# Rotated FFN: the residual added by an accumulating transfer from DRAM instead of by POOL

## The chip, the core and the metric

The kernel runs on one core of a Trainium2 chip. The metric is the device time of one execution in microseconds (us); the time of a kernel is the median of its runs. The engines are named as in the profile: PE (matmul), PEld (its weight loads), DVE (VectorE), ACT (ScalarE), POOL (GpSimd) and SP (SyncE, which only issues transfers here).

## The reference, cut to what matters

The program is one block of a network on `x` of 128 batches of 32 rows of 512 numbers, that is 4096 rows: cross-attention with a residual, then a delta-rule attention block with its own MLP and a residual, and at the end the stage that the change is in, a feed-forward network (FFN) with quantised and Hadamard-rotated activations:

```python
def h_bitlinear(x, w):
    xq = act_quant(fwht(x))      # Hadamard rotation, then 8-bit rounding by the row's maximum
    wq = weight_quant(w)         # weights rounded to -1, 0, 1 times one scale
    return jnp.einsum('bsh,oh->bso', xq, wq)
...
gate = h_bitlinear(hidden_states, w_gate)       # 512 -> 2048
up = h_bitlinear(hidden_states, w_up)           # 512 -> 2048
return h_bitlinear(jax.nn.silu(gate) * up, w_down)   # 2048 -> 512
...
x = x + _L0_ffn_ref(_layernorm(x, axis=-1), L0_ffn_w_gate, L0_ffn_w_up, L0_ffn_w_down)
```

The last line is the one concerned: the `x` ahead of the plus sign is the residual.

## The kernel before, in words

`perceiver_block` runs the stages one after the other: `cross_attention`, `delta_products`, `delta_out_mlp`, `hadamard_ffn`. The MLP stage writes two arrays of 4096 x 512 to DRAM: `x2`, the residual stream, and `z2`, the same rows with their mean taken off and the first part of the Hadamard rotation done. `hadamard_ffn` reads both and writes `out`.

`hadamard_ffn` works on 32 tiles of 128 rows, in a software pipeline of three tiles. In turn `i` of its loop (line 1055) it does, in the order of the program:

- it loads `z` of tile `i+3` (`zt`, four buffers) and turns `z` of tile `i+1` on PE (`turned`, L97, copied by ACT at L970);
- it loads `x2` of tile `i` (`xt`, four buffers) by `load` (L932), through SP's queue;
- it starts the gate and up products of tile `i` (`middle`: PE L996 and L999, ACT's SiLU at L1001, DVE's product at L1002), and between them rounds tile `i+1` (`integers`: DVE's maximum at L976, the scale `qs` by L948 to L951, ACT's rounding `t` at L956, DVE at L960);
- it turns the middle result of tile `i-1` (`middle_turned`), rotates it on PE (`rotated`, L939), finds its maximum (DVE L1016, L1020) and rounds it (`last_integers`, ACT L956 and L958, DVE L960, and the factor `fd` at L1026);
- it turns the integers of tile `i-2` and multiplies them with the last weights (`finish`: 16 matmuls at L1039). ACT scales the product into `xo` (L1041, three buffers), POOL adds `xt` to it (L1042), and a DMA on POOL's queue stores `xo` to `out` (L1043);
- at the end DVE does the rest of the rotation of tile `i`, eight adds and subtractions on 128 x 1024 numbers, ping-pong between the tiles `m` and `mb` (`butterflies`, L126 and L127).

The order in which each engine executes its instructions isn't this order: a scheduler of the language arranges them by priority and by its own estimate of when operands are ready, so that butterflies lie between the short steps of the rounding. Waits between engines, buffers and transfers are made by the language. PSUM has eight buffers in this stage, shared by all products (`ps`). The buffers of a stage are laid on the memory that earlier stages let go, and wait for it tile by tile.

Of the kernel before, what the change touches and what calls it, by code (L numbers as in the profile page):

```python
# [13 lines left out]
ALU = mybir.AluOpType  # L14
# [4 lines left out]
P = 128  # L19
# [99 lines left out]
def butterflies(nc, a, b):  # L119

    n = a.shape[1] // P
    step = 1
    while step < n:
        i = a.rearrange("p (a c d) -> p a c d", c=2, d=step * P)
        o = b.rearrange("p (a c d) -> p a c d", c=2, d=step * P)
        nc.vector.tensor_add(o[:, :, 0, :], i[:, :, 0, :], i[:, :, 1, :])  # L126
        nc.vector.tensor_sub(o[:, :, 1, :], i[:, :, 0, :], i[:, :, 1, :])  # L127
        a, b, step = b, a, 2 * step
    return a
# [769 lines left out]
def hadamard_ffn(g: Ctx, x2, z2, mv2, had, ffn, out):  # L899


    tc, nc = g.tc, g.nc
# [7 lines left out]
    with tc.tile_pool(name="d_w", **right) as wp, tc.tile_pool(name="d_w2", **right) as wp2, stack:  # L910
# [19 lines left out]
        def load(i, src, name):  # L930
            t = xp.tile([P, D], FP, name=name)
            nc.sync.dma_start(t, src[i * P : (i + 1) * P, :])  # L932
            return t

        def rotated(xT, c0):

            pr = ps.tile([P, D], FP, name="ps")
            for c in range(DC):
                nc.tensor.matmul(  # L939
                    pr[:, c * P : (c + 1) * P], xT[:, c0 + c, :], hd, start=True, stop=True  # L940
                )
            return pr
# [19 lines left out]
        def statistics(ns):  # L962

            nc.scalar.activation(rstd[:, ns], mv2[:, ns, 1], AF.Sqrt, bias=g.ln_eps)
            nc.vector.reciprocal(rstd[:, ns], rstd[:, ns])
            nc.vector.tensor_scalar_mul(rstd[:, ns], rstd[:, ns], c1)

        def turned(i):
            zT = wk1.tile([P, DC, P], FP, name="zT")
            nc.scalar.copy(zT, g.transposed(ps, z.pop(i), g.ident))  # L970
            return zT

        def integers(i, pr):

            mx = st.tile([P, 1], FP, name="mx")
            nc.vector.tensor_reduce(mx, pr, AX.X, ALU.max, apply_absolute_value=True)  # L976
            m, qs = scales(mx, rstd[:, i : i + 1])
            q = wk1.tile([P, D], BF, name="q")
            rounded(q, pr, qs)
            f = st.tile([P, 2], FP, name="f")  # L980
            nc.vector.tensor_scalar_mul(f, both, m)
            return q, f

        def integers_turned(q, f):
            qT = wk1.tile([P, DC, P], BF, name="qT")
            nc.scalar.copy(qT, g.transposed(ps, q, g.identb, BF))
            return qT, f

        def middle(qT, f):

            m = mp.tile([P, IF], FP, name="m")
            for k in range(NG):
                ks = slice(k * D, (k + 1) * D)
                pg = ps.tile([P, D], FP, name="ps")
                for dc in range(DC):
                    nc.tensor.matmul(pg, qT[:, dc, :], wg[:, dc, ks], start=dc == 0, stop=dc == DC - 1)  # L996
                pu = ps.tile([P, D], FP, name="ps")
                for dc in range(DC):
                    nc.tensor.matmul(pu, qT[:, dc, :], wu[:, dc, ks], start=dc == 0, stop=dc == DC - 1)  # L999
                s = wk.tile([P, D], FP, name="s")  # L1000
                nc.scalar.activation(s, pg, AF.Silu, scale=f[:, 0:1])  # L1001
                nc.vector.scalar_tensor_tensor(m[:, ks], pu, f[:, 1:2], s, ALU.mult, ALU.mult)  # L1002
                yield m

        def middle_turned(m):
            mT = mp.tile([P, IC, P], FP, name="mT")
            for k in range(NG):
                pt = g.transposed(ps, m[:, k * D : (k + 1) * D], g.ident)
                nc.scalar.copy(mT[:, k * DC : (k + 1) * DC, :], pt)
            return mT  # L1010

        def last_integers(pr):

            mx = st.tile([P, NG], FP, name="mx4")
            for k in range(NG):
                nc.vector.tensor_reduce(  # L1016
                    mx[:, k : k + 1], pr[k], AX.X, ALU.max, apply_absolute_value=True
                )
            mx1 = st.tile([P, 1], FP, name="mx")
            nc.vector.tensor_reduce(mx1, mx, AX.X, ALU.max)  # L1020
            mm, qs = scales(mx1, c2)
            q = mp1.tile([P, IF], BF, name="q2")
            for k in range(NG):
                rounded(q[:, k * D : (k + 1) * D], pr[k], qs, k % 2 == 0)
            f = st.tile([P, 1], FP, name="fd")
            nc.vector.tensor_mul(f, mm, sd)  # L1026
            return q, f

        def last_turned(q):
            qT = mp1.tile([P, IC, P], BF, name="q2T")  # L1030
            for k in range(2):
                pt = g.transposed(ps, q[:, k * IF // 2 : (k + 1) * IF // 2], g.identb, BF)
                nc.scalar.copy(qT[:, k * IC // 2 : (k + 1) * IC // 2, :], pt)  # L1033
            return qT

        def finish(i, x, qT, f):
            pd = ps.tile([P, D], FP, name="ps")
            for c in range(IC):
                nc.tensor.matmul(pd, qT[:, c, :], wd[:, c, :], start=c == 0, stop=c == IC - 1)  # L1039
            xo = wk.tile([P, D], FP, name="xo")  # L1040
            nc.scalar.activation(xo, pd, AF.Copy, scale=f)  # L1041
            nc.gpsimd.tensor_add(xo, xo, x)  # L1042
            nc.gpsimd.dma_start(out[i * P : (i + 1) * P, :], xo)  # L1043

# [2 lines left out]
        rstd = wp.tile([P, n], FP, name="rstd")  # L1049
        z = {i: load(i, z2, "zt") for i in range(3)}  # L1050
        nc.sync.dma_start(wd.rearrange("p c n -> p (c n)"), ffn[2][0])
        x = {}
        statistics(slice(0, late))
        f, m, q = integers_turned(*integers(0, rotated(turned(0), 0))), {}, {}
        for i in range(n + 2):
            if i + 3 < n:
                z[i + 3] = load(i + 3, z2, "zt")
            if i + 1 < n:
                zT = turned(i + 1)
            if i < n:  # L1060
                x[i] = load(i, x2, "xt")
                steps = middle(*f)
                m[i] = next(steps)
            if i == n // 2:
                statistics(slice(late, n))
            if i + 1 < n:
                f = integers(i + 1, rotated(zT, 0))
            if i < n:
                for _ in steps:
                    pass  # L1070
            if 0 <= i - 1 < n:
                mT = middle_turned(m.pop(i - 1))
            if 0 <= i - 2:
                q2, fd = q.pop(i - 2)
                q2T = last_turned(q2)
            if 0 <= i - 1 < n:
                q[i - 1] = last_integers([rotated(mT, k * DC) for k in range(NG)])
            if i + 1 < n:
                f = integers_turned(*f)
            if 0 <= i - 2:  # L1080
                finish(i - 2, x.pop(i - 2), q2T, fd)
            if i < n:
                m[i] = butterflies(nc, m[i], mp.tile([P, IF], FP, name="mb"))

# [2 lines left out]
def perceiver_block(  # L1087
# [26 lines left out]
    with tc.tile_pool(name="s_l", bufs=1, side="right", reuse_waits="tile") as sp:  # L1114
# [9 lines left out]
        def beside_mlp(b):  # L1124
# [9 lines left out]
            x2, z2, mv2, beside_mlp,  # L1134
        )
    hadamard_ffn(g, x2, z2, mv2, had, list(zip(fq, scales)), out)


# [57 lines left out]
```

## Time and profile before

| what | us |
|---|---|
| median of 3 runs | 3079.94 |
| lowest and highest run | 3078.09, 3083.41 |
| the profiled execution | 3080.81 |
| its span | 3079.0 |
| first turn of the FFN on PE | 2414.96 |
| first and last POOL add | 2470.26, 3069.38 |
| PE busy over the whole span | 2934.2 |
| DVE busy over the whole span | 2059.5 |
| ACT busy over the whole span | 1090.1 |
| POOL busy over the whole span | 706.0 |

The span is the profiled execution from its first to its last instruction; the time around it, 1.8 us, is start and end. An engine's busy time is the time in which it executes instructions, without those that issue transfers. In the prediction, a line of a group gives line of code, engine, operation, output and input, count, then busy time and mean time of one, then the idle time of the engine just before these instructions and what ended it. The granted TensorE clock in this execution was 0.984 of full speed over the span.

### The profile page before, as it was taken

Reading aid. Unit: us, or ns where it says so; the run is one execution under the profiler, and the core shown is the slowest. Engines: PE = TensorE matmul, PEld = TensorE weight load, DVE = VectorE, ACT = ScalarE, POOL = GpSimd, SP = SyncE. Lnnn points to the kernel's source line nnn. Section 1 sums busy time; section 2 is a strip of 40 time slices with the busy share of each in tenths; the row PEclk is TensorE's granted clock in tenths of the full one; section 3 lists DMA queues with packets and bytes.
Section 4 is the critical chain, followed back from the end, with each engine's and each line's share of the span. In section 5 each row is a group of like instructions: output and inputs, shape, how many; then the busy total and the mean of one; then the engine's idle time right before and its main releaser. Section 6 shows DMA issues by size and latency. Waiting matters only on the chain.

```text
span 3079.0 us, 42048 instructions
## 1 busy us (share of the span) xinstructions
PE 2934.2 (95%) x15558; PEld 1683.7 (55%) x15558; DVE 2059.5 (67%) x3432; ACT 1090.1 (35%) x1812; POOL 706.0 (23%) x995
## 2 busy tenths in 40 slices
PE   8999999999999999599999999999999899999997
PEld 3444344443333333367676666667777566666664
DVE  2353434326699797378778787878422599999996
ACT  1111111215656666312221112111111366666665
POOL 1121212112686675321212111011000010000001
PEclk9999999999999999799999999999999999999998
DMA  9797989863554544641423323131411111111110
GB/s 332 265 311 269 307 306 310 274 213 98 166 148 131 173 129 132 198 126 59 128 74 106 97 66 112 48 101 50 139 42 42 55 42 42 42 42 35 39 31 21
DMA packets 258236, 408.09 MB, mean 133 GB/s; under 512 B 68336, under 2 KB 170864, under 8 KB 254576
## 3 DMA queue, kind: packets, MB, share of 16 engines
q1 hardware_dynamic: 223856, 305.21, 31.7%
q0 software_dynamic: 34176, 100.19, 9.5%
q8 instruction: 124, 2.03, 0.3%
q14 instruction: 80, 0.66, 0.1%
HBM read 288.36 MB, written 93.85 MB: 124 GB/s over the span
## 4 chain that ended last, share of the span: by engine, by line
PE 41%; DVE 17%; ACT 5%; issue 3%; DMA 2%; SPq 0%; POOL 0%; DVEq 0%; POOLq 0%; ACTq 0%
PE pm L834 9%; PE pm L823 9%; PE pm L826 9%; PE pp L520 5%; PE ps L797 3%; DVE mb L127 3%; ACT t L956 3%; DVE mb L126 2%; DVE mx L1016 2%; DVE m L126 2%; PE pg L455 2%; PE ps L764 2%; DVE m L1002 1%; DVE m L127 1%; DVE W L442 1%
## 5 line engine op out<-in xcount | busy, mean ns | idle before, releaser
L823 PE MATMUL pm<-hT,wg 128*128 128x256 f32 x1408 | 342.1, 386 | 0.7 <-ACT hT L812 0.7
L826 PE MATMUL pm<-hT,wu 128*128 128x256 f32 x1408 | 333.3, 379 | 0.0
L436 DVE TENSOR_TENSOR pr<-L,W 128x1984 f32<-128x1984 f32 (+30 forms) x248 | 312.1, 1258 | 24.6 <-DMA L<-ld 20.6
L442 DVE TENSOR_TENSOR W<-W,pr 128x1984 f32<-128x1984 f32 (+30 forms) x248 | 309.0, 1246 | 3.2
L834 PE MATMUL pm<-wd,mT 128*128 128x512 f32 x704 | 307.2, 592 | 0.0
L823 PEld LDWEIGHTS pm<-hT,wg 128*128 128x128 f32 x1408 | 262.2, 191 | 57.5 <-issue 16.2
L826 PEld LDWEIGHTS pm<-hT,wu 128*128 128x128 f32 x1408 | 267.2, 190 | 36.2
L834 PEld LDWEIGHTS pm<-wd,mT 128*128 128x128 f32 x704 | 132.6, 190 | 160.8 <-issue 160.7
L828 ACT ACTIVATE sg<-pm 128x256 f32<-128x256 f32 x176 | 67.4, 383 | 350.1 <-PE pm L823 340.1
L829 DVE TENSOR_TENSOR mT<-pm,sg 128x256 f32<-128x256 f32 x176 | 73.8, 419 | 164.1 <-PE pm L826 150.0
L1042 POOL TENSOR_TENSOR xo<-xo,xt 128x512 f32<-128x512 f32 x32 | 42.7, 1336 | 581.6 <-ACT xo L1041 581.6
L996 PE MATMUL ps<-wq,qT 128*128 128x512 bf16 x512 | 133.1, 383 | 28.9 <-DVE m L1002 17.3
L956 ACT ACTIVATE t<-ps,magic,qs 128x512 f32<-128x512 f32 x160 | 117.6, 777 | 96.5 <-DVE qs L951 96.4
L461 POOL TENSOR_TENSOR kk<-kk,cm 128x256 f32<-128x256 f32 x128 | 135.5, 1058 | 2.1
L999 PE MATMUL ps<-wq,qT 128*128 128x512 bf16 x512 | 132.4, 381 | 2.2 <-DVE m L1002 2.2
L458 POOL DMA_DIRECT2D ld<-kk x128 | 92.2, 720 | 147.4 <-ACT kk L457 140.4
L346 PE MATMUL ps<-hT,wq 128*128 128x512 f32 x256 | 118.6, 623 | 7.2 <-ACT hT L339 7.2
L939 PE MATMUL ps<-hd,mT 128*128 128x128 f32 x1024 | 121.5, 277 | 0.0
L455 PE MATMUL pg<-kqm,kq 128*32 128x512 f32 x896 | 118.8, 601 | 2.1 <-DMA kqm<-kq 1.5
L302 PE MATMUL ps<-wo,aoT 128*128 128x512 f32 x256 | 118.8, 608 | 1.5 <-ACT aoT L295 1.5
L520 PE MATMUL pp<-hT,wk 128*128 128x512 f32 x256 | 118.6, 604 | 0.3 <-DVE acc L527 0.3
L1039 PE MATMUL ps<-wq,q2T 128*128 128x512 bf16 x512 | 117.2, 383 | 0.9 <-ACT q2T L1033 0.9
(217 smaller groups left out, 5220.6 us busy)
## 6 DMA issues: line engine op xcount, KB each, us to landing
kall<-in_ctxT_dram SPq DMA_DIRECT2D x32, 2056.0 KB
cx<-in_ctx_dram SPq DMA_DIRECT2D x32, 2048.0 KB
x<-xo POOLq DMA_DIRECT2D x64, 256.0 KB, 3.4
xt<-x SPq DMA_DIRECT2D x64, 256.0 KB
ld<-kk POOLq DMA_DIRECT2D x128, 128.0 KB, 2.5
pd<-kk POOLq DMA_DIRECT2D x128, 128.0 KB, 2.3
L<-ld SPq DMA_DIRECT2D x8, 2048.0 KB
pe<-pd SPq DMA_DIRECT2D x256, 64.0 KB
```

The costliest lines, as they stand in the source:

```text
L126: nc.vector.tensor_add(o[:, :, 0, :], i[:, :, 0, :], i[:, :, 1, :])
L436: nc.vector.tensor_mul(pr[:, 0:n], bc(L[:, s, :, s + 1 : T].rearrange("p h t -> p t h"), HD), w[:, s].unsqueeze(1).to_broadcast([P, n, H4, ...
L442: nc.vector.tensor_sub(w[:, s + 1 :], w[:, s + 1 :], pr[:, 0:n])
L455: nc.tensor.matmul(pg[js], k[:, js], m[:, :, :, js], start=True, stop=True)
L461: nc.gpsimd.tensor_mul(kk[:, 1], kk[:, 1], cm.unsqueeze(1).to_broadcast([P, HH, T]))
L520: nc.tensor.matmul(pp.rearrange("p b t -> p (b t)"), w[n][:, dc, ec * P : (ec + 1) * P], hT[:, dc, :], start=dc == 0, stop=dc == DC - 1,)
L823: nc.tensor.matmul(pg, wg[:, dc, fs], hT[:, dc, :], start=dc == 0, stop=dc == DC - 1)
L826: nc.tensor.matmul(pu, wu[:, dc, fs], hT[:, dc, :], start=dc == 0, stop=dc == DC - 1)
L834: nc.tensor.matmul(pd, mT[:, fc, i * P : (i + 1) * P], wd[:, fc, :], start=fc == 0, stop=fc == FC - 1,)
L956: nc.scalar.activation(t, pr, AF.Identity, bias=magic, scale=qs)
L996: nc.tensor.matmul(pg, qT[:, dc, :], wg[:, dc, ks], start=dc == 0, stop=dc == DC - 1)
L999: nc.tensor.matmul(pu, qT[:, dc, :], wu[:, dc, ks], start=dc == 0, stop=dc == DC - 1)
```

## The change

`finish` no longer takes the tile `x`. After ACT has put the scaled product into `xo`, POOL's queue issues a DMA whose source is the tile's rows of `x2` in DRAM and whose destination is `xo` in SBUF, with the operation add: the DMA reads the destination and adds to it. The store of `xo` to `out` is issued by SP's queue instead of POOL's, after that transfer has landed. The add on POOL and the loads of `xt` are gone, and with them the four buffers of `xt`.

```diff
-        def finish(i, x, qT, f):
+        def finish(i, qT, f):
             pd = ps.tile([P, D], FP, name="ps")
             for c in range(IC):
                 nc.tensor.matmul(pd, qT[:, c, :], wd[:, c, :], start=c == 0, stop=c == IC - 1)
             xo = wk.tile([P, D], FP, name="xo")
             nc.scalar.activation(xo, pd, AF.Copy, scale=f)
-            nc.gpsimd.tensor_add(xo, xo, x)
-            nc.gpsimd.dma_start(out[i * P : (i + 1) * P, :], xo)
+            nc.gpsimd.dma_start(xo, x2[i * P : (i + 1) * P, :], accum_op=ALU.add)
+            nc.sync.dma_start(out[i * P : (i + 1) * P, :], xo)
...
-        x = {}
...
-                x[i] = load(i, x2, "xt")
...
-                finish(i - 2, x.pop(i - 2), q2T, fd)
+                finish(i - 2, q2T, fd)
```

## The prediction

> **What bounds the kernel now.** I began with the page's first parts. The span is 3079.0 us; POOL is busy for 23% of it, so its own work cannot be the limit. The line to be changed stands among the costly groups:
>
> ```profile
> L1042 POOL TENSOR_TENSOR xo<-xo,xt 128x512 f32<-128x512 f32 x32 | 42.7, 1336 | 581.6 <-ACT xo L1041 581.6
> ```
>
> It shows 32 adds, one for each tile of 128 rows, 42.7 us in all on an engine that waits 581.6 us for ACT in between. Taken by themselves they are worth nothing. So I asked for the engines' busy time in the steady part of this stage (columns: stretch, its length, then busy us and count of PE, PEld, DVE, ACT, POOL, then the granted clock, DMA share, GB/s):
>
> ```profile
> 2512.00:3032.00 520.00, 490.26 (x3329) 327.38 (x3328) 475.76 (x758) 331.26 (x526) 47.55 (x52) 1.00 0.12 38
> ```
>
> PE and DVE are both above 91% here, the clock is full and the DMA engines are nearly idle. Which of the two leads is told by the chain of waits in order of time, over one tile (start, us, what):
>
> ```profile
> 2567.48 2.21 DVE mb L127
> 2569.69 0.06 DVE m L948
> 2569.76 1.20 DVE m L126
> 2570.95 0.07 DVE qs L950
> 2571.03 0.06 DVE fd L1026
> 2571.09 1.04 issue
> 2572.13 0.16 DVE qs L951
> 2572.29 0.02 issue
> 2572.32 1.45 ACT t L956 x2
> ```
>
> The chain runs through DVE without a break up to the scale `qs`, from there through ACT's rounding `t`, then the SiLU `s`, and back to DVE at L1002. PE is not on it. The "1.04 issue" is no gap: in the timeline DVE runs another butterfly (L127) there. The first line is the odd one: that butterfly took 2.21 us. The groups by shape, from 2500 to 3000 us, show the same instruction against its siblings (busy, mean ns):
>
> ```profile
> L127 DVE TENSOR_TENSOR mb<-m 128x1024 f32<-128x1024 f32 x51 | 88.6, 1738 | 0.0
> L126 DVE TENSOR_TENSOR mb<-m 128x1024 f32<-128x1024 f32 x51 | 62.4, 1223 | 0.9
> L127 DVE TENSOR_TENSOR m<-mb 128x1024 f32<-128x1024 f32 x50 | 60.6, 1213 | 0.0
> ```
>
> A mean of 1738 over 51 is a mixture of 1.22 and 2.29. The timeline says which are long:
>
> ```profile
> 2587.92 1.26 POOL L1042 TENSOR_TENSOR xo<-xo,xt 128x512 f32<-128x512 f32 x1 [18.45 <-ACT xo L1041]
> 2587.97 2.29 DVE L127 TENSOR_TENSOR mb<-m 128x1024 f32<-128x1024 f32 x1
> ...
> 2589.47 0.56 POOL L1043 DMA_DIRECT2D out_dram<-xo  x1 [0.30 <-POOL xo L1042]
> ```
>
> POOL's add ends at 2589.18, and the butterfly ends 1.08 us later, which is its usual time less the overlap of pipelined instructions: it stood still while POOL read SBUF. The POOL adds start at 2488.45, 2508.06, 2527.47, 2548.04 and so on to 3043.78: 28 periods in 555.33 us, a mean of 19.83, made of 11 long ones (20.57) and 17 short ones (19.3 to 19.6). Whether PE has room is in the waits from 2500 to 3000 us (total, times, longest):
>
> ```profile
> PE ps L996 <- DVE m L1002: 17.3, 10, 1.7
> PE ps L996 <- ACT t L956: 9.6, 15, 0.7
> ```
>
> In 25 tiles PE stalls 26.9 us, 1.73 in a long period, about 0.64 in a short one, each time for a PSUM buffer that DVE or ACT releases late. So DVE bounds this stage, through ACT, and PE follows close behind.
>
> **What the Trainium skill says.** "SBUF — State Buffer", section "Who interferes with whom": a DVE instruction with two SBUF inputs and a GpSimd instruction that reads SBUF contend, and the second to issue is blocked fully until the first is done. The trace agrees: 2.29 against 1.22 us, and the order of issue is as stated (POOL 0.05 us ahead). The same section separates DMA from engine ports: DMA traffic contends with no engine, while writing the descriptors of a GpSimd DMA does need SBUF. The trace shows plain issues at L1043 (0.56 us each) beside butterflies that kept their 1.22 us. "DMA: Bandwidth & Descriptors", section "SWDGE vs HWDGE vs iDMA", says that only GpSimd issues an accumulating DMA; no such transfer is in this trace. Its section "Rules for kernel authors" says that an accumulate reads its destination and writes later, so others must wait for its semaphore: the store of `xo` therefore waits for it to land.
>
> **The change part by part.**
>
> *Removed: 32 POOL adds.* On POOL: 42.7 us, off the chain, worth 0. On DVE: the butterflies held, those of the adds from 2488.45 to 3023.11, are 28, at 2.29 - 1.22 = 1.07 us; 28 x 1.07 = 30.0. At 3043.78 the add holds L1026 instead, which takes 1.14 in place of 0.14: 1.0. The first add (2470.26) was itself the one that waited, and at the last two (3062.53, 3069.38) DVE is not in a butterfly. Sum 31.0 us, each on the chain. How much comes through? In a long period PE's stall falls from 1.73 to 0.7, so all 1.07 comes through. In a short one PE can move up only 0.64 at L996; but then its turns of `m` (L97) wait three times more for ACT, 0.23, 0.16 and 0.16 us in the timeline, 0.55 in all, which ACT's earlier `t` and `s` take away too. 0.64 + 0.55 = 1.19 is just over 1.07. I take 95%: -29.5, bounds -22 (first rival) to -31.
>
> *Removed: 32 loads of `xt` on SP*, 0.32 us of queue each, waiting for the add: worth 0, nothing waited for SP.
>
> *Added: 32 accumulating DMAs on POOL in the place of 32 plain stores.* Each waits for ACT's `xo`, as the add did; behind it on POOL is only the next tile's. `x2` was last stored at 2416.14, landing 5.2 later, before the first use at 2470. Steady cost 0 if the issue is like L1043. Unknown from both sides: from 0, if it holds nothing, to a hold of its whole length on DVE, which is the slower rival. The issue moves 1.5 us earlier, beside the same butterfly as the add; I take 0, since plain issues held none.
>
> *Moved: 32 stores from POOL to SP*, 0.32 us of queue each. SP now waits for the accumulate to land, and the next load of `zt` stands behind that wait. A `zt` buffer is one of four and is filled some three periods (59 us) before use; 8 us late costs 0. Who else waits: ACT's `xo` has three buffers; a buffer lives 0.7 + 1.7 + 3.2 = 5.6 us now, and with a landing of 4 about 0.7 + 4.3 + 3.5 = 8.5 us, of 59. That cover would be gone only at a landing above some 50 us.
>
> *The end.* Now: ACT ends `xo` at 3069.29, POOL adds, issues at 3070.93, and lands 3.2 later at 3074.1; the close-down takes the rest to 3079.0. After: issue at 3069.5; landing unknown, from 2.3 (the page's row for `z` stores) to 10.4 (its 1088 KB row); a 256 KB store to `x2` has 3.4, and I choose 4.0, since this transfer also reads what it adds to. 3073.5, SP 0.3, landing 3.2: 3077.0. That is +2.9; bounds +0.2 to +9.5.
>
> *The start.* Four `xt` buffers leave the pool, so tiles behind it lie 8 KB lower and may fall on other tiles of the MLP stage. The last of those is let go by the store at 2419.20, landing 4.1 later, 2423.3, and the first product here is at 2415: between -1 and +8; I take 0, since the first turns need only `zt`, allocated ahead of `xt`.
>
> *The order of instructions* is a scheduler's; the long and short periods differ by one butterfly ahead of L951. All short: 11 x 1.25 = -14. All long: 17 x 1.25 = +21. I take 0, because DVE's work and its data don't change.
>
> Sum: -29.5 + 2.9 = -26.6. The profiled execution took 3080.81 (span 3079.0 and 1.8 around it), so it would become 3054.2; the median shown, 3079.94, lies 0.9 lower: **3053.5 us**.
>
> **The rivals.** *PE takes over.* Only the visible stalls can go: 11 x 1.07 + 17 x 0.64 = 22.7, less 2.9: -19.8, 3060. For it: PE is busy 94%. Against it: the hidden waits at L97. *The order turns out differently*: 3040 with all periods short, 3053.5 + 21 = 3074.5 with all long. For it: small changes of timing in a scheduler move such choices. Against it: POOL and SP gate no DVE instruction. *Slower: the accumulating issue holds DVE.* Place: POOL's issue right behind `xo`, beside L127. If writing its descriptors shuts DVE out for its whole length, the cost is 31 x that length; it eats the gain of 26.6 at 0.9 us and makes the kernel measurably slower (+6.2) from about 1.1 us. At 2 us: 62 - 26.6 = +35, 3115. For it: the accumulating form is in no row and may need more descriptors. Against it: 32 plain issues held nothing.
>
> **How the numbers follow.** Forecast 0.57, PE takes over 0.19, shorter order 0.08, longer order 0.07, issue holds DVE 0.09. About 0.2%, 6.2 us, is what a measurement can tell from no change. Faster: 0.57 + 0.19 + 0.08 = 0.84; same: 0.07; slower: 0.09. The range runs from 3043, most of the way to the shorter order, to 3075, the longer order with the bounds of start and end in the forecast; the slower rival stays out.
>
> **What would show it.** Right: L127 `mb` at a mean near 1220 ns, periods near 18.3 and 19.5, PE stalls at L996 down to about 0.7 and 0, no `xt`, a tail that ends some 8 us after the last `xo`. PE takes over: DVE waits for `ps` at L1016 or L1002, PE without stalls, periods of 18.7. Wrong: L127 still long beside POOL's DMA issue; or periods unchanged with L127 short, which would say that something else than DVE set them.

## The result and the profile after

The changed kernel takes 3048.1 us (median of 4 runs, 3047.4 to 3048.8) against 3081.7 for the kernel before in the same series (3078.1 to 3083.6). The ratio is 0.9892, with a 95% interval from 0.9876 to 0.9907: 33.6 us faster by the medians. The profiled execution took 3048.66, its span is 3046.9.

The page has the line of the change first (columns as before). POOL has no add left; what L1042 now counts is the issue of a transfer:

```profile
L1042 POOL DMA_DIRECT2D xo<-x x32 | 27.1, 848 | 591.1 <-ACT xo L1041 591.1
```

An issue of the accumulating form takes 0.85 us, where the plain store at L1043 took 0.56 before. The groups by shape, from 2500 to 3000 us, are those that told of the stall before:

```profile
L126 DVE TENSOR_TENSOR mb<-m 128x1024 f32<-128x1024 f32 x54 | 66.1, 1224 | 0.9
L127 DVE TENSOR_TENSOR mb<-m 128x1024 f32<-128x1024 f32 x54 | 65.8, 1218 | 0.0
L127 DVE TENSOR_TENSOR m<-mb 128x1024 f32<-128x1024 f32 x54 | 65.7, 1217 | 0.0
```

The mixed mean of 1738 ns is gone: L127 into `mb` is as fast as its siblings. The count says the rest: 54 in 500 us in the place of 51. In the timeline the same butterfly stands beside POOL's issue and keeps its 1.21 us, in either order:

```profile
2584.80 1.21 DVE L127 TENSOR_TENSOR mb<-m 128x1024 f32<-128x1024 f32 x1
...
2584.90 0.83 POOL L1042 DMA_DIRECT2D xo<-x  x1 [18.65 <-ACT xo L1041]
...
2603.14 0.85 POOL L1042 DMA_DIRECT2D xo<-x  x1 [17.40 <-ACT xo L1041]
2603.15 1.21 DVE L127 TENSOR_TENSOR mb<-m 128x1024 f32<-128x1024 f32 x1
```

In the first pair the butterfly starts ahead of the issue, in the second behind it; neither is held.

The waits of the same stretch (total, times, longest) show what became of PE's stalls:

```profile
PE ps L996 <- DVE m L1002: 5.9, 9, 0.7
```

Before, PE stood 26.9 us there in 25 tiles. Now the short periods have no stall and the long ones 0.65 us. In the steady stretch (stretch, length, then PE, PEld, DVE, ACT, POOL, clock, DMA, GB/s) PE is busy for 98%:

```profile
2512.00:2992.00 480.00, 471.30 (x3241) 323.82 (x3290) 438.25 (x742) 325.42 (x516) 21.16 (x25) 1.00 0.18 41
```

From the fifth period on, a period (from one start of ACT's `xo` to the next) is shorter by the hold and by no more: the short and the long ones take 18.23 and 19.49 us where they took 19.31 and 20.57. PE, DVE and ACT execute the same instructions in the same order in both kernels (some 60 of PE's 4096 matmuls are missing from the later trace), so nothing of this comes from a new order. The chain of waits, useful before, is not so here: at the end it follows POOL's issues, and most of their idle time is put down to "issue".

Where the 33.1 us between the two spans' FFN stages (664.1 and 630.9, from PE's first turn of `zt` to the end of the span) lie, by the starts of `xo` (the 0.69 us of the last `xo` itself are left out):

| part | before | after | difference |
|---|---|---|---|
| PE's first turn to the first `xo` | 54.54 | 56.71 | +2.2 |
| first to thirtieth `xo`, 29 periods | 573.51 | 541.67 | -31.8 |
| thirtieth to last `xo` | 25.60 | 22.85 | -2.8 |
| end of the last `xo` to the end of the span | 9.76 | 9.01 | -0.7 |

The stage is the better measure for small differences: in the profiles of all kernels here it begins anywhere from 2405 to 2421 us, though no instruction ahead of it was changed (one kernel writes the residual stream to another place).

### The profile page after: what moved, and what is told of

Same layout as the page of the kernel before. It is cut to its first block, busy times and chain, and to the rows that moved or that the text cites. A ratio compares the mean times of both kernels' runs of the same rounds, so it can differ in the third digit from the quotient of the medians.

```text
span 3046.9 us, 41948 instructions
## 1 busy us (share of the span) xinstructions
PE 2924.9 (96%) x15496; PEld 1685.1 (55%) x15558; DVE 2030.7 (67%) x3432; ACT 1090.5 (36%) x1812; POOL 660.0 (22%) x963
## 4 chain that ended last, share of the span: by engine, by line
PE 39%; issue 23%; DVE 3%; DMA 1%; POOL 1%; ACT 0%; SPq 0%; POOLq 0%; DVEq 0%; ACTq 0%
PE pm L823 8%; PE pm L834 8%; PE pm L826 8%; PE pp L520 5%; PE ps L797 4%; PE pg L455 2%; PE ps L764 2%; DVE W L442 1%; DVE pr L436 1%; POOL xo L1042 1%; DMA wd<-in_WdownT_dram 1%; PE ps L97 1%; PE pm L455 0%; PE pn L579 0%; DMA xs<-x 0%
## 5 line engine op out<-in xcount | busy, mean ns | idle before, releaser
L1042 POOL DMA_DIRECT2D xo<-x x32 | 27.1, 848 | 591.1 <-ACT xo L1041 591.1
L996 PE MATMUL ps<-wq,qT 128*128 128x512 bf16 x509 | 131.7, 380 | 8.3 <-DVE m L1002 5.9
L999 PE MATMUL ps<-wq,qT 128*128 128x512 bf16 x484 | 126.2, 381 | 1.1 <-DVE m L1002 1.1
L520 PE MATMUL pp<-hT,wq 128*128 128x512 f32 x256 | 116.9, 598 | 0.0
```

The source lines that it names most:

```text
L520: nc.tensor.matmul(pp.rearrange("p b t -> p (b t)"), w[n][:, dc, ec * P : (ec + 1) * P], hT[:, dc, :], start=dc == 0, stop=dc == DC - 1,)
```

## The experiments

My theory: POOL's add read SBUF beside a two-input butterfly of DVE and held it, about 1.07 us in each tile, on the path that set the period. The first rival: the queues, that is the loads of `xt`, the store, or the transfers' place, made the difference. The second: any POOL work there holds DVE.

**The store alone on SP.** The kernel before with

```diff
-            nc.gpsimd.dma_start(out[i * P : (i + 1) * P, :], xo)
+            nc.sync.dma_start(out[i * P : (i + 1) * P, :], xo)
```

> The kernel before with one part of the change alone: the store of xo is issued by SP, the POOL add and the xt loads stay. Theory (POOL's read of SBUF holds DVE's butterfly): the long L127 stays in every tile, time as before, 3081.7 within 4 us; the end may move by up to 3 us, since the last transfer now hangs on SP. Rival (it is the queues: POOL's or SP's transfers were in the way): most of the 33.6 us appears here, about 3050.

Ratio 0.9987 (0.9976 to 0.9998), medians 3074.6 against 3079.4. L127 `mb` has a mean of 1746 ns, the periods are 19.31 and 20.56 as before, the stage lasts 662.9 us. From the first to the thirtieth `xo` it takes 572.4 us against 573.5. By the stage the move of the store is worth about 1 us of 33 (by the medians, in which the start of the stage varies too, 4.8 of 33.6). The end is 3.2 us shorter, 6.6 after the last `xo`, but the start and the last tiles took 3.1 longer.

**The add back, and nothing else.** The changed kernel with a dummy tile of ones and

```diff
+            scr = wk.tile([P, D], FP, name="scr", bufs=1)
+            nc.gpsimd.tensor_add(scr, xo, dummy)
             nc.gpsimd.dma_start(xo, x2[i * P : (i + 1) * P, :], accum_op=ALU.add)
```

> The changed kernel, and ahead of its accumulating transfer one POOL add per tile of the same size as the old one (two SBUF tiles of 128x512 into a scratch tile that nobody uses); transfers stay as changed. Theory: the butterfly is held again, L127 mb at a mean near 1740 ns, 31 us come back: 3048.1 + 31 = 3079. Rival (the gain came from the loads, the store or the accumulating transfer): 3048 to 3050, the add hides on POOL.

Ratio to before 0.9990 (0.9982 to 0.9999): the gain is gone but for some 3 us. The groups by shape:

```profile
L127 DVE TENSOR_TENSOR mb<-m 128x1024 f32<-128x1024 f32 x51 | 87.7, 1719 | 0.0
L1045 POOL TENSOR_TENSOR scr<-xo,dummy 128x512 f32<-128x512 f32 x25 | 32.1, 1282 | 433.6 <-ACT xo L1043 433.6
```

The mean period is 19.74 again, 1.06 above the changed kernel's 18.68. The accumulating transfer, the store on SP and the missing loads are all still in this kernel, so none of them is the cause. An add that nobody uses costs 30.7 us over 29 periods, on an engine that idles for most of the stage.

**POOL busy, but writing.**

```diff
+            scr = wk.tile([P, 2 * D], FP, name="scr", bufs=1)
+            nc.gpsimd.tensor_add(scr[:, 0:1], xo[:, 0:1], magic)
+            nc.gpsimd.memset(scr, 0.0)
             nc.gpsimd.dma_start(xo, x2[i * P : (i + 1) * P, :], accum_op=ALU.add)
```

> The changed kernel, and at the same place on POOL one element per partition added (to tie it to xo) and then a memset of 128x1024 of a scratch tile: POOL is busy about as long as with the add, but reads next to nothing. Theory (it is the reading of SBUF by POOL that holds DVE): L127 mb stays near 1220 ns, time 3048 to 3051. Rival (any POOL work beside the butterfly holds DVE): as with the add, near 3079.

Ratio 0.9899 (0.9878 to 0.9921), mean period 18.68: no cost. The timeline shows more than was asked:

```profile
2561.02 1.22 DVE L127 TENSOR_TENSOR mb<-m 128x1024 f32<-128x1024 f32 x1
2561.03 1.25 POOL L1043 TENSOR_TENSOR scr<-xo,magic 128x1 f32<-128x1 f32 x1 [15.18 <-ACT xo L1041]
2562.34 0.95 POOL L1044 MEMSET scr<- 128x1024 f32 x1
...
2598.75 0.18 POOL L1043 TENSOR_TENSOR scr<-xo,magic 128x1 f32<-128x1 f32 x1 [15.18 <-ACT xo L1041]
2598.86 1.22 DVE L127 TENSOR_TENSOR mb<-m 128x1024 f32<-128x1024 f32 x1
2598.99 0.95 POOL L1044 MEMSET scr<- 128x1024 f32 x1
```

In the first case DVE was 0.01 us ahead, and POOL's one-element read took 1.25 us, the length of the butterfly; in the second POOL was ahead and took 0.18. Together with the held butterflies of before: whoever starts second waits, in both directions. The memset of 0.95 us lies wholly inside the second butterfly, which keeps its 1.22. This settles the second rival: it is the reading. It also shows that the time of POOL's issue is not the cause: here the transfer is issued 1.3 us or more after the end of `xo`, in place of 0.3, and nothing is lost.

**Two adds.** As the add back, with a second line `nc.gpsimd.tensor_add(scr, scr, dummy)`.

> As e2 with two POOL adds per tile one behind the other. Theory: the second add holds DVE too. If it goes ahead of the waiting butterfly, the loss doubles (1.07 + 1.26 = 2.3 us a tile, about 3048 + 69 = 3117); if DVE gets its turn between the two, POOL waits and the next butterfly is held in part, 3085 to 3110. Rival: 3048 to 3050.

3106.65 us, ratio 1.0096 (1.0075 to 1.0118); the mean period is 20.67, 2.0 above the changed kernel's. The timeline of a tile where both hold DVE:

```profile
2629.42 1.26 POOL L1045 TENSOR_TENSOR scr<-xo,dummy 128x512 f32<-128x512 f32 x1 [16.06 <-ACT xo L1043]
2629.46 2.31 DVE L127 TENSOR_TENSOR mb<-m 128x1024 f32<-128x1024 f32 x1
2630.76 2.13 POOL L1046 TENSOR_TENSOR scr<-scr,dummy 128x512 f32<-128x512 f32 x1
2631.80 2.17 DVE L126 TENSOR_TENSOR m<-mb 128x1024 f32<-128x1024 f32 x1
```

They take turns: add, butterfly, add, butterfly, each waiting for the other. In other tiles one of the two adds holds not a butterfly but the short product of two inputs that makes `fd` (1.15 us in place of 0.14), so that its mean is a mixture as well:

```profile
L1028 DVE TENSOR_TENSOR fd<-m,sc 128x1 f32<-128x1 f32 x24 | 17.7, 738 | 0.0
```

In each tile from the second to the thirtieth DVE is thus held twice, for 2.0 us in all, and that is what the period grows by; the time is within the range given. The same sum can be made for each kernel that has the add: how much longer than usual (1.22 us for a butterfly, 0.14 for `fd`) DVE's held instructions took between the first and the thirtieth `xo`, beside what these 29 periods took more than in the changed kernel.

| kernel | holds | sum of the holds, us | 29 periods longer by, us |
|---|---|---|---|
| before | 29 | 30.6 | 31.8 |
| store alone on SP | 29 | 30.5 | 30.7 |
| add back | 29 | 29.6 | 30.7 |
| two adds | 57 | 58.3 | 57.7 |
| changed | 0 | 0 | 0 |

So nearly all of a hold comes through to the period, in each of them.

**Store on POOL behind the accumulate.**

```diff
-            nc.sync.dma_start(out[i * P : (i + 1) * P, :], xo)
+            nc.gpsimd.dma_start(out[i * P : (i + 1) * P, :], xo)
```

> The changed kernel with the store of xo on POOL's queue behind the accumulating transfer instead of on SP's. Theory: in the steady tiles nothing waits for either queue, so 3048 within 3 us; the end tells whether the short close-down (9.0 us after the last xo, although a transfer was added) belongs to the store on SP: if it does, the end grows by about 3 us here, 3051. Rival (POOL waiting for the landing, 4.3 us a tile, gets in the way of the next tile): periods longer than 18.2, 3060 or more.

3048.3, ratio 0.9893 (0.9872 to 0.9914), mean period 18.68, stage 631.1 against 630.9. POOL waits for each landing, and nothing is late. The end is 9.6 us after the last `xo` against 9.0, not 12: the short close-down does not belong to the store on SP. Which queue stores is indifferent.

**No residual.** `xo` is stored by POOL as ACT leaves it; the residual is left out.

> The changed kernel without the residual: the accumulating transfer is left out, xo is stored by POOL as it comes from ACT. What is left is the floor of this stage without any price for the residual. Theory (the accumulating transfer costs only at the end): 3048 less about 4 us of landing = 3044, steady periods 18.2 and 19.5 as in the changed kernel. Rival (the accumulating transfer's 0.85 us issue or its traffic still holds DVE or PE somewhat): periods shorter by 0.1 us or more, 3041 or less.

3040.9, ratio 0.9871 (0.9853 to 0.9889), but the stage lasts 630.4 us, 0.6 less than in the changed kernel, and the mean period is 18.67: the rest of the difference in the medians lies ahead of the stage, and the intervals of the two ratios overlap. The accumulating transfers, 32 of 256 KB, are free in the steady tiles to within 0.01 us a tile, and my 4 us at the end were wrong: without that landing the program closes 8.7 us after the last `xo`, only 0.3 earlier.

**One transfer in place of two.** The MLP stage writes the residual stream into the output (`x2 = out`), and `finish` only does

```diff
-            nc.gpsimd.dma_start(xo, x2[i * P : (i + 1) * P, :], accum_op=ALU.add)
-            nc.sync.dma_start(out[i * P : (i + 1) * P, :], xo)
+            nc.gpsimd.dma_start(out[i * P : (i + 1) * P, :], xo, accum_op=ALU.add)
```

> A version that might beat both: the MLP stage writes the residual stream straight into the output array, and xo is added to it there by one accumulating transfer from SBUF to DRAM per tile; no second transfer. Theory: steady tiles unchanged, the end loses the second transfer: 4.3 us or a little less, 3044 to 3046. Rival (accumulating into DRAM lands much later than into SBUF, over 8 us): no gain, 3048 or more.

3050.75, ratio 0.9895 (0.9870 to 0.9919), stage 631.6: no gain. The rival's reason is wrong too, since accumulating into DRAM lands after a median of 4.3 us, as into SBUF. What ends the kernel must be something else. The closing instructions of the changed kernel (queue, kind, count: shortest, median, longest ns, first to last start) show it:

```profile
L1190 POOLq DRAIN  x3: 46/98/7652, 3038.2 to 3046.6; - x3
L1190 SPq DRAIN  x3: 7/7/7, 3044.6 to 3046.4; - x3
```

SP is through at 3044.6, when the last store has landed. POOL's first DRAIN starts with its last DMA issue at 3038.2 and takes 7.65 us, to 3045.8, and only then is the program closed. The kernel before has the same, later and with more time lost:

```profile
L1192 POOLq DRAIN  x3: 40/102/7363, 3070.9 to 3078.8; - x3
L1192 SPq DRAIN  x3: 7/7/7, 3073.8 to 3078.5; - x3
```

There the store had landed by 3073.8, and the close waited until 3078.3. Without the residual, with the accumulate into DRAM and with the adds back, too, the DRAIN ends 7.3 to 7.7 us after the start of POOL's last DMA.

**One DVE step to ACT.** `rounded(q, pr, qs, True)` in `integers`.

> The changed kernel with the first rounding's second step (L960 of the next tile, 0.43 us of DVE) on ACT instead (0.72 us): what binds after the change? If DVE still leads, up to 0.4 us a tile go, 3048 - 12 = 3036; if PE leads now in the short periods, only the long ones (11 of 28) gain, about -4; if ACT's part of the loop leads, it gets slower by up to 0.7 us a tile, 3070. The order on DVE and ACT changes here, so a few us more or less may come from that.

3044.4, ratio 0.9877 (0.9857 to 0.9897), but the stage takes 631.7 us and the mean period is 18.67: no gain. From the fourth on all periods are equal, 18.76, in the place of 18.23 and 19.49 (18.73 on the average from the fifth on). PE is busy for 476.7 of 480 us, against 471.3, and has no stall at the gate product L996 left; its weight loads wait for DVE at the turns of `m` (L97), 9.5 us in 500. Taking 0.43 us from DVE buys nothing on the average. It looks as if PE leads here, but no run shows it.

**Another end.** For the last two tiles, with `xl` loaded early,

```diff
-            nc.scalar.activation(xo, pd, AF.Copy, scale=f)
-            nc.gpsimd.dma_start(xo, x2[i * P : (i + 1) * P, :], accum_op=ALU.add)
+            if i in last:
+                nc.vector.scalar_tensor_tensor(xo, pd, f, last[i], ALU.mult, ALU.add)
+            else:
+                nc.scalar.activation(xo, pd, AF.Copy, scale=f)
+                nc.gpsimd.dma_start(xo, x2[i * P : (i + 1) * P, :], accum_op=ALU.add)
```

> The changed kernel with another end: for the last two tiles the residual is loaded early and DVE scales and adds in one instruction from PSUM, and SP stores; the other 30 tiles use the accumulating transfer. In ten profiles but two the close-down waited for POOL's DRAIN, which ended 7.3 to 7.7 us after POOL's last DMA issue began, whatever the last transfer was. Theory (the end hangs on POOL's last DMA): POOL's last DMA comes 23 us earlier, the end is then the SP store of the last tile, some 5 us after the last product in place of 9.7: 3048 - 4.5 = 3043.5. Rival (the DRAIN belongs to the end of the program, not to POOL's DMA): the DRAIN stays long and the end stays near 9 us, 3047 to 3049.

3034.1, ratio 0.9864 (0.9843 to 0.9884); the changed kernel beside it has 0.9893, so the intervals overlap. The stage tells it more sharply: 625.5 us against 631.0, 5.5 less. POOL's DRAIN is over long before the end:

```profile
L1196 POOLq DRAIN  x3: 98/194/7487, 3007.2 to 3032.6; - x3
L1196 SPq DRAIN  x3: 7/7/7, 3031.8 to 3032.1; - x3
```

It runs from 3007.2 to 3014.7, and the program closes 1.3 us after the last store has landed (3031.8 to 3033.1), 3.8 us after the last `xo` in place of 9.0. That the end hung on POOL's DRAIN, and that it comes earlier when POOL's last work does, is shown. That this work must be a DMA is not: with the store alone on SP, POOL's last DMA starts at 2421.4 and its last work is the add at 3073.5, and yet

```profile
L1192 POOLq DRAIN  x3: 40/102/5482, 3073.4 to 3079.7; - x3
L1192 SPq DRAIN  x3: 7/7/7, 3076.9 to 3079.2; - x3
```

POOL's DRAIN takes 5.5 us and ends 2.0 us after SP is through.

**The changed kernel again**, on that chip:

> The changed kernel as it is, on the same chip as e9, e10 and e11, so that those can be set against it and not only against the kernel before: ratio to before 0.989, first xo to thirtieth xo 541.7 us, end 9.0 us after the last xo.

3044.0, ratio 0.9893 (0.9873 to 0.9913), 541.5 us from the first to the thirtieth `xo`, stage 631.0, end 9.1 after the last `xo`.

**Less work for DVE.** `butterflies` stops a step early, so that part of the rotation is missing.

> The changed kernel without the last of the four steps of the butterflies (two of eight DVE instructions of 1.22 us, so part of the rotation is left out): what binds after the change? If DVE still leads all through, 2.3 us a tile go, 16.4 a tile, 3048 - 66 = 2982. If PE stands right behind (it stalls only 0.65 us in the long periods and none in the short ones), the mean period falls from 18.68 to about 18.1 and no further, 3048 - 17 = 3031. The order of instructions changes a little here.

3146.9, ratio 1.0227 (1.0199 to 1.0254): 25% of the butterflies less, and some 100 us slower. Neither number came near. The scheduler's order changed more than I thought: the timeline of a tile shows ACT doing the next tile's `zT` only behind the roundings of the last one, and PE standing for it:

```profile
2615.35 0.59 ACT L970 COPY zT<-ps 128x512 f32<-128x512 f32 x1
...
2615.99 1.58 PE L939 MATMUL ps<-hd,zT 128*128 128x128 f32 x8 [3.28 <-ACT zT L970]
```

In 500 us PE waits 73.2 us there. The granted clock in this stage falls to 0.93 to 0.95 as well, and the two are not told apart. The question which engine binds next is not answered by this run; it does suggest that a change of the order can cost more than the change that this document is about gains.

**The add on DVE.** The kernel before with

```diff
-            nc.scalar.activation(xo, pd, AF.Copy, scale=f)
-            nc.gpsimd.tensor_add(xo, xo, x)
+            nc.vector.scalar_tensor_tensor(xo, pd, f, x, ALU.mult, ALU.add)
```

> The kernel before with the residual added by DVE (one instruction from PSUM that scales and adds, about 0.75 us, in the place of ACT's 0.69 us and POOL's add); xt loads and the store on POOL stay. No POOL read beside DVE, but 0.75 us of work more on DVE. Theory (DVE's time is what counts in each tile): the gain is the difference, (1.08 - 0.75) x 29 = 10 us, 3070, give or take the new order of instructions. Rival (holding POOL away is all that counts, DVE has room for 0.75 us): 3048.

3038.55, ratio 0.9878 (0.9855 to 0.9902), stage 624.7 us, 6.3 less than the changed kernel's, mean period 18.58. The forecast of 3070 failed, and with it the theory as I had put it for this run, that DVE's time is what counts: DVE works more (455.0 us in 480, against 438.3) and the stage is faster. DVE had idle time, 34.1 us in the changed kernel's 500 waiting for ACT's `t` at L960, and only 17.5 are left here. I read it so: what cost was not DVE's sum of work but a stop between the maximum and `qs`, for which ACT waits (76.6 us in 500 before, 50.4 in the changed kernel, 44.5 here). That isn't shown by itself: ACT's 0.69 us that go, and the new order, are in the number as well, and are not told apart.

Two versions with the residual thus have a shorter stage than the changed kernel, this one and the one with another end, though the intervals of their whole times overlap with its own. The two ideas together were not run.

## Why the prediction was right

The prediction was 3053.5 with a range of 3043 to 3075; measured were 3048.1. By its steps:

- **What bounds.** Right as to the path: the hold lay on it in each steady tile, and short and long periods lost 1.08 and 1.08 us, as the prediction's 18.3 and 19.5 had it. The removal of the hold gives 30.7 us over 29 periods (19.736 with the add back against 18.678). "DVE bounds this stage" doesn't hold for DVE's sum of work: with 0.43 us less of it nothing was gained, and with the add on DVE the stage was 6.3 us shorter.
- **How much comes through.** I took 95%, -29.5. It was all of it and a little more, -31.8: 30.7 come from the add, the other 1.1 are there with the store alone on SP. The working missed one hold: behind the first add, at 2471.43, another butterfly took 2.23. The second to fourth periods alone gained 1.43, 1.23 and 1.58 us, and lost 1.34, 1.19 and 1.53 again with the add back; why these are more than 1.07 was not tried. The first rival, PE taking over, would have kept the short periods at 18.7; they are 18.23 to 18.36. But the sum 0.64 + 0.55 that stood against it was misread: the wait of 0.23 at L97 is in the long periods alone, where it stays, and the short ones had only two of 0.16. In a short period PE's third gate product comes 4.34 us after the first in place of 5.13, so 0.79 sooner where the visible stall was 0.64, and the turns of `m` take 1.97 in place of 2.26: 0.79 + 0.29 = 1.08. That PE's room just covered the hold was luck. PE has no stall left in these periods.
- **The accumulating issue.** Taken at 0 beside DVE: right, though it is longer than a plain one (0.85 against 0.56 us). The slower rival needed a hold of DVE for the issue's length; the butterfly beside it keeps 1.21 us, whichever starts first. The ground for the 0 was thinner than the prediction says: of the 32 plain issues one, at 3046.03, lay beside a butterfly of 1.21, and 29 lay in the rest of the butterfly that the add had held, which still ended 1.08 us after the add.
- **The landing.** Taken as 4.0 us, measured 4.3 (median).
- **The end.** Wrong: +2.9 forecast, -0.7 measured. The step that failed is "lands 3.2 later at 3074.1; the close-down takes the rest". I let the close-down follow the last landing at a fixed distance (3.2 was the median, too; before, the last store had landed by 3073.8). It follows POOL's DRAIN, which began at 3070.9 before and 3038.2 after; against the last `xo`, POOL's issue comes 1.35 us earlier than it did, the DRAIN is 0.3 longer and what follows it another 0.3, and the second transfer lies in its shade. The bounds were mis-summed as well: landings of 2.3 and 10.4 in the place of 4.0 give +1.2 and +9.3, not +0.2 and +9.5, and -0.7 is outside either.
- **The start and the last tiles.** Taken at 0: +2.2 and -2.8. In both PE ran part of the time at a lower clock. The last product took 5.11 us before and 3.63 after, and between 2400 and 2470 us the granted clock was 0.98 before and 0.93 after. In the other experiments the start took 55.0 to 57.6 us (52.2 with the short rotation) and, where the accumulating transfer was kept, the last tiles 22.3 to 25.5. I can't name the cause of the phase of the clock; that the two terms nearly cancel is luck.
- **Order.** Taken as unchanged: right, exactly.
- **The sum.** 3054.2 less 0.9 is 3053.3, not 3053.5. For the profiled execution the forecast of 3054.2 was 5.5 too long: 2.3 us in the steady tiles, 3.6 at the end, 0.6 at the start and in the last tiles together, less 1.0 by which the stage began later.

The Trainium skill's rule in "SBUF — State Buffer", section "Who interferes with whom", carried the forecast, and the runs agree with it: reading holds (2.29 against 1.22 us), writing doesn't (1.22 beside the memset), and the second to start waits, POOL too (1.25 us for one element). No run here varies the number of inputs of DVE's instruction.

## What to carry to other kernels

Look for one instruction that has two durations in one group: a mean far from its siblings' may be a mixture, and the timeline beside another engine shows what could hold it. An engine that is far from busy can cost time where it reads SBUF beside a two-input DVE instruction on the path; moving its sum into a transfer cost nothing here, where the transfer was off the path. What is won is then the hold itself, where it stands on the path, and not the sum of work of the engine that was held.

## What the runs showed of the hardware that I had not expected

- POOL's add and DVE's butterfly take turns: a second add in a row did not go ahead of a waiting butterfly (1.26, 2.31, 2.13, 2.17 us), and in each steady tile both adds held DVE.
- An accumulating DMA of 256 KB costs POOL 0.85 us of issue and lands after 4.3 us (median), from DRAM into SBUF and from SBUF into DRAM alike (medians of 3.9 to 4.4 over the kernels); a plain store from POOL before took 0.56 and 3.2 (medians of 2.3 to 3.3).
- POOL's DRAIN at the end of the program ends 7.3 to 7.7 us after the start of its last DMA's issue in 12 of the 14 profiles, plain or accumulating, also where the data landed up to 5 us earlier. Two differ: with the store on POOL behind the wait for the accumulate its DRAIN took 2.75 us, and with the store alone on SP, where no DMA of POOL was near, 5.5. What it waits for is open.
